# Score columns gathered behind the second half of a projection, one clip per tile, and the first stage's Relu placed behind other copies

## The chip, the cores and the metric

The kernel runs on one core of one Trainium2 chip. A core has five engines that run side by side, each with its own instruction queue: TensorE (PE in the profile; PEld is its weight load), VectorE (DVE), ScalarE (ACT), GpSimd (POOL) and SyncE (SP), which here only issues transfers. ScalarE and GpSimd issue transfers too. The metric is the device time of one execution in microseconds; lower is better.

## What is computed

Four graph layers over 3327 nodes with 512 features each, and one adjacency matrix `adj` for all. Every layer normalises its input, applies a Relu, and adds the layer's output to its input. Layers 0 to 2 are attention layers (8, 4 and 8 heads), layer 3 is a mean over neighbours. An attention layer, cut to what matters here:

```python
h  = maximum(layernorm(x), 0)
Wh = h @ W                          # per head: 64 or 128 columns
s1 = (Wh * a1).sum(-1)              # per node and head
s2 = (Wh * a2).sum(-1)
e  = leaky_relu(s1[:, None] + s2[None, :], 0.2)
x  = x + elu(softmax(where(adj > 0, e, -inf)) @ Wh)
```

The scores s1 and s2 are linear in h, so the kernel folds the vectors a1 and a2 into extra columns of the weight matrix ("score columns"): one projection of a tile of nodes gives Wh and both scores of every head.

## The kernel before, in words

**Tiles and stages.** The nodes lie in 26 tiles of 128. A first stage (to about 150 us) takes layer 0's tiles through normalisation and projection. Then three attention stages follow, each over 7 chunks of four tiles and all heads; the tiles of the next layer are normalised and projected in between, as each chunk gets done, by the same functions. Layer 3 ends it.

**Order.** The program is written as if one thing followed another; a scheduler places the instructions of each engine in an order of its own, from the dependencies and from priorities by place in the source, before the kernel runs. On the chip each engine then goes through its list in that order. The helper `after(inst, name)` (line 145) adds a dependency for the scheduler alone: `inst` has to be placed behind the named instruction. It adds no wait by itself, but the engine's order carries it.

**A tile's steps in the first stage** (`node_stages`, line 530, with `first=True`; line numbers as in the profile):

- load of x (L153, issued from ScalarE's queue); statistics on VectorE (L349, L353), three small operations on GpSimd (L354 to L356);
- Relu with scale and bias on ScalarE, giving `h` (L362);
- four transposes on TensorE into `tp` (L138), a copy on ScalarE into `hT` (L142);
- the projection on TensorE (L418), eight matmuls, into two PSUM tiles `acc` of four that there are: each half `f` of the heads has 256 columns of Wh and 2 x 4 score columns of its own, 264 in all. For tiles 0 and 1 the score columns are made later, by 128x8 matmuls, as their folding (L334, L338) ends late;
- a clip of the scores, one for each half, from PSUM into `s12` on VectorE (L438); two exponentials on ScalarE (L449, L452);
- two multiplications on VectorE (L457), each of one half of Wh with the exponentials, giving `AB`; they free the PSUM tiles;
- `pieces`: AB is split into three bf16 numbers. First pieces are copied on ScalarE (L393, two), the rest `r` is AB minus these, on VectorE (L389), second pieces are copied on ScalarE (L402, two), third pieces are subtracted on GpSimd (L400, two); then they are stored (L410, L411).

The stage is run by a hook that calls one step of each tile in flight, the oldest first. So in one hook run the Relu of tile t + 3 comes after the pieces of tile t in the source. Beside it run the mask steps for the first chunk: a load and cast of `adj` from GpSimd's queue (L227), transposes on TensorE (L235), a comparison on VectorE (L245), a store; and, in the scheduler's gaps, comparison matrices for the first head (L689 on ScalarE, L686, L693 and L695 on VectorE). The attention's matmuls are L804 and L807 (L797 and L800 in layer 1), the last layer's L1073.

**The Relu's place.** In the first stage `relu()` calls `normed` with no named instruction, as `behind()` gives nothing while no attention has run.

Of the kernel before, what the change touches and what calls it, by code (L numbers as in the profile page):

```python
# [25 lines left out]
F32 = mybir.dt.float32  # L26
# [6 lines left out]
ALU = mybir.AluOpType  # L33
# [4 lines left out]
P = 128  # L38
# [14 lines left out]
def tile_gnn(ctx: ExitStack, tc: tile.TileContext, x, adj, W0, a01, W1, al, ar, W2, a2,  # L53
# [91 lines left out]
    def after(inst, name):  # L145

        tc.add_manual_dep(inst.ins, name, mybir.DependencyInfo(mybir.DependencyClass.NoSync,
                                                               mybir.DependencyReason.SCHED_ONLY))
# [10 lines left out]
    stats = []  # L159
    scales = []  # L160
    copied = []

# [132 lines left out]
    def open_layer(l):  # L297
        L = Layer()
        L.l = l
        L.to_store = []  # L300
        if l == 3:
            L.w = []
            for i in range(2):
                w = pre.tile([P, KC, 2 * WW], F32, name="w")[:, :, :D]
                after(nc.sync.dma_start(w, Xd[i].rearrange("(c p) o -> p c o", p=P)), stored["gate"])
                L.w.append(w)
            return L
        H = heads[l]
        DK = D // H
        H2 = H // 2  # L310

        w = pre.tile([P, KC, 2 * WW], F32, name="w")[:, :, :2 * (D // 2 + H)]
        L.w = w.rearrange("p c (f o) -> p c f o", f=2)
        av = []
        for i in range(2):
            av.append(pre.tile([P, 2, H2, DK], F32, name="h"))
            ld = (nc.sync if l or i == 0 else nc.scalar).dma_start(av[i].rearrange("p f h d -> p (f h) d"),
                                                                   a_srcs[l][i].partition_broadcast(P))
            if l:
                after(ld, stored["gate"])  # L320
        for k in range(KC):
            for f in range(2):
                dst = L.w[:, k, f, :D // 2]
                if l == 0:
                    (nc.scalar if f else nc.sync).dma_start(dst.rearrange("p (g o) -> p g o", g=H2),
                                      W0[f * H2:(f + 1) * H2, k * P:(k + 1) * P, :].rearrange("h p o -> p h o"))
                else:
                    W = (W1, W2)[l - 1]
                    ld = nc.sync.dma_start(dst, W[k * P:(k + 1) * P, f * (D // 2):(f + 1) * (D // 2)])  # L329
                    if l:  # L330
                        after(ld, stored["gate"])
        def fold(i, k):
            pr = pre.tile([P, 2, H2, DK], F32, name="e" if l or i else "AB", bufs=1)
            m = (nc.gpsimd if l == 0 and i else nc.vector).tensor_mul(  # L334
                pr, L.w[:, k, :, :D // 2].rearrange("p f (g o) -> p f g o", g=H2), av[i])
            if gone or i:
                after(m, gone[-1] if gone else relus[1])
            nc.vector.tensor_reduce(L.w[:, k, :, D // 2 + i * H2:D // 2 + (i + 1) * H2], pr, AX.X, ALU.add)  # L338
        hooks.small = [lambda i=i, k=k: fold(i, k) for k in range(KC) for i in range(2)]
        L.ks2 = pre.tile([P, NT, H], F32, name="ks2")  # L340
        L.ns2 = pre.tile([P, NT, H], F32, name="ns2")
        L.s12 = pre.tile([P, 2, NT, H], F32, name="s12", bufs=1)
        nc.vector.memset(L.s12, 0.0)
        return L
# [15 lines left out]
    def normed(xt, mv, pool, behind=None):  # L360
        h = pool.tile([P, D], F32, name="h", bufs=2)
        act = nc.scalar.activation(h, xt, AF.Relu, bias=mv[:, 3:4], scale=mv[:, 2:3])  # L362
        if behind:
            after(act, behind)
        relus.append(act.ins.name)
        return h

    def high(v):

        b = v.bitcast(BF16)  # L370
        names = "abcd"[:len(v.shape) - 1]
        return b.rearrange(f"p {' '.join(names[:-1])} ({names[-1]} two) -> p {' '.join(names)} two", two=2)[..., 1]

    def pieces(L, t, AB, pool, first, behind=None):

        l = L.l
        g, jj = jwhere[t]
        H, DA, AO, HW = dims(l)

        o, two = (t % 2, 2) if first else (0, 1)  # L380
        if o == 0:
            L.pt = pool.tile([P, H, 2, two, AO] if l == 1 else [P, H, two, HW], BF16, name="pt", bufs=3 if first else 2)
        pt = L.pt
        def dst(s, a):
            if l == 1:
                return pt[:, :, a, o, s * DA:(s + 1) * DA]
            return pt[:, :, o, a * AO + s * DA:a * AO + (s + 1) * DA]
        r = pool.tile([P, 2, H, DA], F32, name="r", bufs=2 if first else 1)
        sb = nc.vector.tensor_sub(r, AB, high(AB))  # L389
        if behind:  # L390
            after(sb, behind)
        for a in range(2):
            cp = nc.scalar.copy(dst(0, a), high(AB[:, a]))  # L393
            if behind:
                after(cp, behind)
        ones = nc.gpsimd.memset(pt[:, :, :, o, 3 * DA:AO] if l == 1 else
                                pt[:, :, o].rearrange("p h (a w) -> p h a w", a=2)[..., 3 * DA:AO], 1.0)
        after(ones, cp.ins.name)
        for a in range(2):
            nc.gpsimd.tensor_sub(dst(2, a), r[:, a], high(r[:, a]))  # L400
        for a in range(2):
            nc.scalar.copy(dst(1, a), high(r[:, a]))  # L402
        js = slice(jj + 1 - two, jj + 1)
        if o == two - 1 and l == 1:
            for a in range(2):
                L.to_store.append((abd[l][g][:, a, :, js, :].rearrange("h p j w -> p h j w"), pt[:, :, a]))
        elif first and o == two - 1:
            if g not in ahead:
                ahead[g] = pieces_tile(L, bp, g)
            nc.sync.dma_start(ahead[g][:, js], pt[:, 0])  # L410
            stored[t] = nc.sync.dma_start(abd[l][g][:, :, js, :].rearrange("h p j w -> p h j w"), pt).ins.name  # L411
        elif o == two - 1:
            L.to_store.append((abd[l][g][:, :, js, :].rearrange("h p j w -> p h j w"), pt))

    def products(L, pws, hT, o, e):
        for f, pw in enumerate(pws):
            for k in range(KC):
                mm = nc.tensor.matmul(pw[:, o:e], hT[:, k, :], L.w[:, k, f, o:e], start=(k == 0), stop=(k == KC - 1))  # L418
                if o and k == 0:
                    after(mm, L.mm)  # L420
                L.mm = mm.ins.name

    def projected(L, t, hT, first, pws=None):


        l, n = L.l, pn(t)
        H, DA, AO, HW = dims(l)
        H2 = H // 2
        full = D // 2 + H
        if pws:  # L430
            products(L, pws, hT, D // 2, full)
        else:
            pws = [(accs if first else ps).tile([P, full], F32, name="acc" if first else "mm") for f in range(2)]
            products(L, pws, hT, 0, D // 2 if first and t < 2 else full)
            if first and t < 2:
                return pws
        for f, pw in enumerate(pws):
            nc.vector.tensor_scalar(L.s12[:n, :, t, f * H2:(f + 1) * H2],  # L438
                                    pw[:n, D // 2:].rearrange("p (i h) -> p i h", i=2), -S_CLIP, S_CLIP,
                                    op0=ALU.max, op1=ALU.min)  # L440
        return pws

    def scaled(L, t, pws, pool, first, behind=None):

        H, DA, AO, HW = dims(L.l)
        DK, H2 = DA - 1, H // 2
        s2 = L.s12[:, 1, t, :]
        AB = pool.tile([P, 2, H, DA], F32, name="AB", bufs=2 if first else 1)
        ex = nc.scalar.activation(AB[:, 0, :, DK], s2, AF.Exp)  # L449
        if behind:  # L450
            after(ex, behind)
        ex = nc.scalar.activation(AB[:, 1, :, DK], s2, AF.Exp, scale=SLOPE)  # L452
        if behind:
            after(ex, behind)
        for f in range(2):
            hs = slice(f * H2, (f + 1) * H2)
            nc.vector.tensor_mul(AB[:, :, hs, :DK],  # L457
                                 pws[f][:, None, :D // 2].rearrange("p a (h d) -> p a h d", h=H2).to_broadcast([P, 2, H2, DK]),
                                 AB[:, :, hs, DK:DA].to_broadcast([P, 2, H2, DK]))
        return AB  # L460
# [69 lines left out]
    def node_stages(L, t, get_x, pool, first=False):  # L530
# [9 lines left out]

        def relu():

            q["h"] = normed(q["x"], q["mv"], pool, copied[-1] if t == NT - 1 and not first else behind())

        def turn():
            b = L.mm if t == NT - 1 and not first else behind()
# [990 lines left out]
```

## Time and profile before

| | |
|---|---|
| three runs | 3469.95, 3473.6, 3474.15 us; median 3473.6 |
| the profiled execution | 3468.92 us, span 3467.1 us, granted clock of TensorE 0.996 |
| first and last L418 into `acc` (first stage) | 10.1 and 150.8 us |
| first L804 | 151.02 us |
| L457 in the first stage | 26.34 us (tiles 0 and 1) to 154.88 us (tile 25), 0.68 us each |
| L362, mean from 40 to 130 us | 0.81 us |
| L393 and L402, mean of one there | 0.63 us |
| L389, mean there | 1.33 us |
| L400, mean of one there | 1.08 us |
| L438, all of the kernel | 156 of them, some 0.155 us each |

How to read it: the span is the time from the first to the last instruction of one execution that the hardware profiler recorded; the execution's own time has a little around it. A duration in a row includes the engine's latency, so that neighbours on one engine overlap by about 0.1 us. A wait in square brackets is the idle time of the engine just before an instruction, and who ended it. Each projection matmul stands as two records, since float32 goes through TensorE in two passes.

### The profile page before, as it was taken

Reading aid. Unit: us, or ns where it says so; the run is one execution under the profiler, and the core shown is the slowest. Engines: PE = TensorE matmul, PEld = TensorE weight load, DVE = VectorE, ACT = ScalarE, POOL = GpSimd, SP = SyncE. Lnnn points to the kernel's source line nnn. Section 1 sums busy time; section 2 is a strip of 40 time slices with the busy share of each in tenths; the row PEclk is TensorE's granted clock in tenths of the full one; section 3 lists DMA queues with packets and bytes.
Section 4 is the critical chain, followed back from the end, with each engine's and each line's share of the span. In section 5 each row is a group of like instructions: output and inputs, shape, how many; then the busy total and the mean of one; then the engine's idle time right before and its main releaser. Section 6 shows DMA issues by size and latency. Waiting matters only on the chain.

```text
span 3467.1 us, 77643 instructions
## 1 busy us (share of the span) xinstructions
PE 3413.3 (98%) x30751; PEld 3092.9 (89%) x30751; DVE 2638.6 (76%) x5209; ACT 2503.5 (72%) x4125; POOL 640.1 (18%) x894
## 2 busy tenths in 40 slices
PE   8899999999999999999999999999999999999999
PEld 6799999999999788888888879989898989887887
DVE  7889888888878799889988877877776768682221
ACT  6778888878878888888888767766676757582211
POOL 7611222212111202223223320000000001021000
PEclk9999999999999999999999999999999999999999
DMA  8799999999857887887777876555555555486331
GB/s 229 239 294 280 239 265 264 254 271 258 240 186 269 282 290 260 283 277 267 278 271 267 334 271 201 190 189 164 192 174 179 187 175 186 166 299 263 103 110 55
DMA packets 398117, 797.70 MB, mean 230 GB/s; under 512 B 112969, under 2 KB 221844, under 8 KB 397104
## 3 DMA queue, kind: packets, MB, share of 16 engines
q1 hardware_dynamic: 363890, 723.14, 64.9%
q0 software_dynamic: 28128, 62.42, 7.3%
q10 hardware_dynamic: 5726, 7.08, 0.7%
q8 instruction: 245, 4.01, 0.5%
q14 instruction: 128, 1.05, 0.1%
HBM read 663.59 MB, written 129.64 MB: 229 GB/s over the span
## 4 chain that ended last, share of the span: by engine, by line
PE 89%; DMA 3%; DVE 2%; ACT 2%; SPq 1%; issue 0%; POOL 0%; POOLq 0%; DVEq 0%
PE acc L807 25%; PE acc L804 25%; PE acc L797 13%; PE acc L1073 9%; PE acc L800 5%; PE mm L493 5%; PE mm L418 5%; ACT gt L689 1%; PE tp L138 1%; DMA ab<-ab 1%; DMA tr<-at 1%; PE mm L191 1%; DMA ab<-pt 0%; DVE AB L457 0%; SPq L329 0%
## 5 line engine op out<-in xcount | busy, mean ns | idle before, releaser
L689 ACT ACTIVATE gt<-s1b,ks 128x512 fp8e4<-128x512 f32 (+1 forms) x2448 | 1448.4, 677 | 374.8 <-PE acc L807 262.2
L804 PE MATMUL acc<-ab,tht 128*128 128x195 bf16 (+1 forms) x9112 | 1551.8, 248 | 2.4 <-DVE deg L825 1.4
L807 PE MATMUL acc<-ab,gt 128*128 128x195 bf16 (+1 forms) x9112 | 1550.8, 248 | 1.5 <-DVE gt L695 1.5
L807 PEld LDWEIGHTS <-gt 128*128 128x128 fp8e4 x10744 | 1052.2, 98 | 21.4 <-issue 15.4
L804 PEld LDWEIGHTS <-tht 128*128 128x128 fp8e4 x10744 | 1052.3, 98 | 17.2 <-issue 5.8
L693 DVE TENSOR_TENSOR tht<-gt,m 128x768 uint32<-128x768 uint32 (+3 forms) x557 | 448.4, 805 | 100.5 <-ACT gt L689 98.1
L695 DVE TENSOR_TENSOR gt<-tht,m 128x768 uint32<-128x768 uint32 (+3 forms) x557 | 447.3, 803 | 9.5
L658 ACT CAST ts<-tht 128x1536 fp32r<-128x1536 fp8e4 x208 | 302.1, 1471 | 95.9 <-PE acc L797 89.3
L686 DVE TENSOR_SCALAR gt<-s1b,ns 128x512 fp8e4<-128x512 f32 (+1 forms) x446 | 223.7, 505 | 166.7 <-PE acc L807 165.9
L797 PE MATMUL acc<-ab,ts 128*128 128x258 f32 x2496 | 333.1, 289 | 0.2
L797 PEld LDWEIGHTS acc<-ab,ts 128*128 128x128 f32 x2496 | 312.1, 189 | 8.4 <-issue 0.8
L921 POOL TENSOR_TENSOR xt<-xt,e 128x512 f32<-128x512 f32 x72 | 121.2, 1684 | 1047.4 <-DVE e L920 988.5
L689 ACT ACTIVATE tht<-s1b,ks 128x512 fp8e4<-128x512 f32 (+1 forms) x504 | 309.1, 680 | 0.7
L1073 PE MATMUL acc<-y,mf 128*128 128x512 f32 x1352 | 309.6, 391 | 0.0
L1073 PEld LDWEIGHTS acc<-y,mf 128*128 128x128 f32 x1352 | 253.6, 188 | 55.8 <-issue 0.5
L804 PE MATMUL acc<-abx,tht 128*128 128x195 bf16 (+1 forms) x1632 | 283.0, 248 | 1.6 <-DVE tht L693 1.6
L807 PE MATMUL acc<-abx,gt 128*128 128x195 bf16 (+1 forms) x1632 | 283.0, 248 | 0.8 <-DVE rc L842 0.8
L822 DVE TENSOR_REDUCE R<-acc 128x130 f32<-128x390 f32 x416 | 214.7, 555 | 77.8 <-PE acc L807 77.0
L1070 ACT CAST mf<-m 128x768 fp32r<-128x768 fp8e4 (+1 forms) x78 | 59.1, 762 | 243.2 <-PE acc L1073 231.4
L800 PE MATMUL acc<-ab,tht 128*128 128x387 bf16 x1248 | 225.4, 329 | 6.8 <-DMA ab<-ab 5.6
L797 PE MATMUL acc<-ab,tv 128*128 128x258 f32 x1664 | 217.9, 283 | 0.7 <-DMA ab<-ab 0.7
L797 PEld LDWEIGHTS acc<-ab,tv 128*128 128x128 f32 x1664 | 206.9, 189 | 1.4 <-DVE e L905 0.9
(168 smaller groups left out, 3721.9 us busy)
## 6 DMA issues: line engine op xcount, KB each, us to landing
ab<-ab SPq DMA_DIRECT2D x333, 600.0 KB, 5.8
ab<-ab SPq DMA_DIRECT2D x112, 774.0 KB, 6.7
ab<-ab SPq DMA_DIRECT2D x112, 516.0 KB, 5.6
ab<-ab SPq DMA_DIRECT2D x112, 400.0 KB, 3.8
abx<-ab SPq DMA_DIRECT2D x110, 400.0 KB, 6.6
ab<-ab SPq DMA_DIRECT2D x56, 582.0 KB, 6.2
s1b<-s SPq DMA_DIRECT2D x120, 256.0 KB, 5.4
m<-mask SPq DMA_DIRECT2D x69, 384.0 KB, 4.3
```

The lines of the kernel that those rows point to most:

```text
L418: mm = nc.tensor.matmul(pw[:, o:e], hT[:, k, :], L.w[:, k, f, o:e], start=(k == 0), stop=(k == KC - 1))
L658: (nc.scalar.copy if KIND[g] == "s" else nc.vector.tensor_copy)(t[:, :k1 - k0, :nj], th[a][g][:, k0:k1])
L686: nc.vector.tensor_scalar(gv[:, :, jj, :], s1v, L.ns2[:, j, h:h + 1], 2.0, op0=ALU.is_gt, op1=ALU.mult, saturate=False)
L689: nc.scalar.activation(gv[:, :, jj, :], s1v, AF.Relu, bias=L.ks2[:, j, h:h + 1], scale=BIG, saturate=False)
L693: nc.vector.tensor_tensor(pu, gu, mu, ALU.bitwise_and)
L695: nc.vector.tensor_tensor(gu, pu, mu, ALU.bitwise_xor)
L797: mm = nc.tensor.matmul(acc[k][:, :2 * DA], thr[g][:, k - ks[0], jj, :], ab[a][g][:, jj, :], start=(j == 0), stop=(j == NT - 1), skip_grou ...
L800: mm = nc.tensor.matmul(acc[k][:, :3 * DA], th[a][g][:, k, jj, :], ab[a][g][:, jj, :3 * DA], start=(j == 0), stop=(j == NT - 1), skip_grou ...
L804: nc.tensor.matmul(acc[k][:, :3 * DA + o], th[0][g][:, k, jj, :], ab[0][g][:, jj, :3 * DA + o], start=(j == 0), stop=False, skip_group_che ...
L807: mm = nc.tensor.matmul(acc[k][:, AO:AO + 3 * DA + o], th[1][g][:, k, jj, :], ab[0][g][:, jj, AO:AO + 3 * DA + o], start=False, stop=(j == ...
L822: nc.vector.tensor_reduce(R[:, k], v.rearrange("p a (s d) -> p a d s", s=3), AX.X, ALU.add)
L1073: nc.tensor.matmul(acc[k], mf[:, jj, :], y2[g][:, jj, s, :], start=(j0 + jj == 0 and s == 0), stop=(j0 + jj == NT - 1 and s == 1))
```

## The change

Three things are done together.

1. The score columns of all heads stand behind the second half's 256 columns of Wh instead of behind each half's own. The second half becomes 256 + 2 x 8 = 272 columns wide (264 in layer 1 with 4 heads), the first half 256. The weights' layout in SBUF follows, and so does the folding of a1 and a2 (L338).
2. The second half is projected first, then the first half, and the multiplications L457 follow that order. All scores are clipped by one instruction per tile. For tiles 0 and 1 the score columns are one group of four matmuls of 16 columns each instead of two of four with 8 columns.
3. In the first stage the Relu gets a scheduling dependency: it is placed behind the last copy of second pieces (L402) that stands ahead of it in the source.

```diff
@@ open_layer
-        w = pre.tile([P, KC, 2 * WW], F32, name="w")[:, :, :2 * (D // 2 + H)]
-        L.w = w.rearrange("p c (f o) -> p c f o", f=2)
+        L.w = pre.tile([P, KC, 2 * WW], F32, name="w")
...
-                dst = L.w[:, k, f, :D // 2]
+                dst = L.w[:, k, f * (D // 2):(f + 1) * (D // 2)]
...
-            nc.vector.tensor_reduce(L.w[:, k, :, D // 2 + i * H2:D // 2 + (i + 1) * H2], pr, AX.X, ALU.add)
+            nc.vector.tensor_reduce(L.w[:, k, D + i * H:D + (i + 1) * H].rearrange("p (f g) -> p f g", f=2), pr, AX.X,
+                                    ALU.add)
@@ pieces
         for a in range(2):
-            nc.scalar.copy(dst(1, a), high(r[:, a]))
+            cp = nc.scalar.copy(dst(1, a), high(r[:, a]))
+        pieced.append(cp.ins.name)
@@ products, projected
-    def products(L, pws, hT, o, e):
-        for f, pw in enumerate(pws):
-            for k in range(KC):
-                mm = nc.tensor.matmul(pw[:, o:e], hT[:, k, :], L.w[:, k, f, o:e], start=(k == 0), stop=(k == KC - 1))
-                if o and k == 0:
-                    after(mm, L.mm)
-                L.mm = mm.ins.name
+    def products(L, pw, hT, o, e, behind=None):
+        for k in range(KC):
+            mm = nc.tensor.matmul(pw, hT[:, k, :], L.w[:, k, o:e], start=(k == 0), stop=(k == KC - 1))
+            if behind and k == 0:
+                after(mm, behind)
+            L.mm = mm.ins.name
...
         if pws:
-            products(L, pws, hT, D // 2, full)
+            products(L, pws[1][:, DH2:], hT, D, D + 2 * H, L.mm)
         else:
-            pws = [(accs if first else ps).tile([P, full], F32, name="acc" if first else "mm") for f in range(2)]
-            products(L, pws, hT, 0, D // 2 if first and t < 2 else full)
+            pws = [(accs if first else ps).tile([P, DH2 + 2 * H * f], F32, name="acc" if first else "mm")
+                   for f in range(2)]
+            if first and t < 2:
+                products(L, pws[1][:, :DH2], hT, DH2, D)
+            else:
+                products(L, pws[1], hT, DH2, D + 2 * H)
+            products(L, pws[0], hT, 0, DH2)
             if first and t < 2:
                 return pws
-        for f, pw in enumerate(pws):
-            nc.vector.tensor_scalar(L.s12[:n, :, t, f * H2:(f + 1) * H2],
-                                    pw[:n, D // 2:].rearrange("p (i h) -> p i h", i=2), -S_CLIP, S_CLIP,
-                                    op0=ALU.max, op1=ALU.min)
+        nc.vector.tensor_scalar(L.s12[:n, :, t, :], pws[1][:n, DH2:].rearrange("p (i h) -> p i h", i=2),
+                                -S_CLIP, S_CLIP, op0=ALU.max, op1=ALU.min)
@@ scaled
-        for f in range(2):
+        for f in (1, 0):
@@ node_stages, relu
-            q["h"] = normed(q["x"], q["mv"], pool, copied[-1] if t == NT - 1 and not first else behind())
+            b = (pieced[-1] if pieced else None) if first else copied[-1] if t == NT - 1 else behind()
+            q["h"] = normed(q["x"], q["mv"], pool, b)
```

In the built program the Relus of tiles 2 and 3 stand behind the second pieces of tile 1, and from then on that of tile t + 3 behind those of tile t. In the order that the build gives, ScalarE's list for a tile in the first stage changes from

```
exponentials(t+1), copy hT, Relu(t+4), load, first pieces(t+1), second pieces(t+1)
```

to

```
first pieces(t), second pieces(t), Relu(t+3), load, exponentials(t+1), copy hT, first pieces(t+1)
```

and in some groups two tiles' exponentials stand together ahead of both tiles' pieces. VectorE's list moves the mask comparison from before the multiplications to between them and `r` in most tiles, and has one clip fewer per tile; the first mask loads on GpSimd stand behind the third pieces of tiles 0 and 1. On TensorE the transposes of tiles 2 and 3 keep their place behind the score columns of tiles 0 and 1. From the attention on, the lists are the same but for the projection's shapes, the missing clips, and a few neighbours that change places where a layer ends.

More of the change, by code (lines that the diff above doesn't have):

```diff
@@ L161, in tile_gnn @@
     copied = []
+    pieced = []
     WW = D // 2 + 8
@@ L334, in fold @@
             m = (nc.gpsimd if l == 0 and i else nc.vector).tensor_mul(
-                pr, L.w[:, k, :, :D // 2].rearrange("p f (g o) -> p f g o", g=H2), av[i])
+                pr, L.w[:, k, :D].rearrange("p (f g o) -> p f g o", f=2, g=H2), av[i])
             if gone or i:
                 after(m, gone[-1] if gone else relus[1])
-            nc.vector.tensor_reduce(L.w[:, k, :, D // 2 + i * H2:D // 2 + (i + 1) * H2], pr, AX.X, ALU.add)
+            nc.vector.tensor_reduce(L.w[:, k, D + i * H:D + (i + 1) * H].rearrange("p (f g) -> p f g", f=2), pr, AX.X,
+                                    ALU.add)
         hooks.small = [lambda i=i, k=k: fold(i, k) for k in range(KC) for i in range(2)]
@@ L428, in projected @@
         H2 = H // 2
-        full = D // 2 + H
+        DH2 = D // 2
         if pws:
-            products(L, pws, hT, D // 2, full)
+            products(L, pws[1][:, DH2:], hT, D, D + 2 * H, L.mm)
         else:
-            pws = [(accs if first else ps).tile([P, full], F32, name="acc" if first else "mm") for f in range(2)]
-            products(L, pws, hT, 0, D // 2 if first and t < 2 else full)
+            pws = [(accs if first else ps).tile([P, DH2 + 2 * H * f], F32, name="acc" if first else "mm")
[5 more added lines that the diff above has]
+            products(L, pws[0], hT, 0, DH2)
             if first and t < 2:
                 return pws
-        for f, pw in enumerate(pws):
-            nc.vector.tensor_scalar(L.s12[:n, :, t, f * H2:(f + 1) * H2],
-                                    pw[:n, D // 2:].rearrange("p (i h) -> p i h", i=2), -S_CLIP, S_CLIP,
-                                    op0=ALU.max, op1=ALU.min)
+        nc.vector.tensor_scalar(L.s12[:n, :, t, :], pws[1][:n, DH2:].rearrange("p (i h) -> p i h", i=2),
+                                -S_CLIP, S_CLIP, op0=ALU.max, op1=ALU.min)
         return pws
```

## The prediction

> **What bounds the kernel now.** I read the busy shares first, then the windows by stage, then the timeline of one tile and the waits of TensorE. The page:
>
> ```profile
> PE 3413.3 (98%) x30751; PEld 3092.9 (89%) x30751; DVE 2638.6 (76%) x5209; ACT 2503.5 (72%) x4125; POOL 640.1 (18%) x894
> DVE  7889888888878799889988877877776768682221
> POOL 7611222212111202223223320000000001021000
> PE 89%; DMA 3%; DVE 2%; ACT 2%; SPq 1%; issue 0%; POOL 0%; POOLq 0%; DVEq 0%
> ```
>
> TensorE sets the time over the whole, but not at the start, where POOL's first digits are 7 and 6. The windows (TensorE, weight loads, VectorE, ScalarE, GpSimd, then clock, DMA share, GB/s):
>
> ```profile
> 60.00:90.00 30.00, 26.67 (x153) 21.64 (x153) 28.05 (x50) 24.55 (x55) 26.64 (x39) 1.00 0.92 273
> 90.00:120.00 30.00, 26.50 (x143) 21.69 (x143) 29.23 (x55) 25.75 (x56) 27.10 (x47) 1.00 0.90 272
> 120.00:150.00 30.00, 25.06 (x118) 20.27 (x117) 22.60 (x42) 21.11 (x50) 19.87 (x29) 0.89 0.57 193
> 400.00:1000.00 600.00, 600.00 (x6723) 591.40 (x6721) 518.73 (x1036) 497.67 (x847) 117.07 (x181) 1.00 0.96 250
> ```
>
> Up to 150 us, the first stage, VectorE is the fullest engine (28 to 29 of 30 us) and TensorE waits. From 400 to 1000 us TensorE has no idle time. So the change can pay or cost only where the first stage hands over to the attention, at 151.02 us, when L804 first runs. One tile's turn in that stage, from the timeline (start, duration):
>
> ```profile
> 62.69 1.24 DVE L389 TENSOR_TENSOR r<-AB 128x1040 f32<-128x1040 f32 x1
> 63.96 1.16 ACT L402 COPY pt<-r 128x520 bf16<-128x520 bf16 x2
> 64.52 0.94 DVE L245 TENSOR_SCALAR m<-tp 128x768 fp8e4<-128x768 bf16 x1
> 65.18 0.21 ACT L449 ACTIVATE AB<-s 128x8 f32<-128x8 f32 x1
> 65.52 1.29 DVE L457 TENSOR_TENSOR AB<-acc,AB 128x512 f32<-128x512 f32 x2
> 65.85 0.81 ACT L362 ACTIVATE h<-xt,mv 128x512 f32<-128x512 f32 x1
> ```
>
> The subtraction r ends at 63.93, ScalarE copies the second pieces, makes the next tile's exponentials, and VectorE multiplies at 65.52, 1.59 us after r; between them it had the statistics and the mask comparison to do and waited for nothing. The Relu comes after the exponentials. The whole list of multiplication pairs runs from 35.31 (tile 2) to 141.47 (tile 22): 106.2 us for 20 tiles.
>
> **The parts that cost nearly nothing.** Projection columns: eight matmuls of 264 become four of 272 and four of 256, 2112 columns either way, and a tile's take 3.53 us in the chain of waits: difference 0 (layer 1 likewise, 2080 columns from eight of 260 or four each of 264 and 256). One clip replaces two per tile, 78 fewer: at 0.155 us (median row of L438) 12 us of VectorE. 52 of them lie in layers 1 and 2 beside a TensorE without idle time: 0; if that cover were gone, 8 us. The other 26 are 4 us of the first stage, taken into the working below. A clip of twice the width appears in no row; the 8 elements per partition take 0.13 to 0.17 us, so 0.15 up to twice that; I take 0.15, by the row nearest in size. The shuffles elsewhere in the built order (one tile's copies two places earlier, a DMA past its neighbour on SP's queue) touch windows where TensorE idles 14 us in 2000 (1000 to 3000): between -2 and +2, taken as 0. For tiles 0 and 1, the score columns take 8 matmuls for 16, which is 16 records fewer at 4.09/26 = 0.157 us, 2.5 us of TensorE. That would let tile 2's transposes start earlier, but they now wait for something else.
>
> **The Relu, at the start.** It moves behind the second copies of the tile three back (of tile 1 for tiles 2 and 3). Queued behind it on ScalarE: the transposed copy, the next exponentials, hence VectorE's multiplication; behind it on TensorE, the transposes and all that follows them in order.
>
> ```profile
> 22.13 4.09 PE L418 MATMUL acc<-w,hT 128*128 128x8 f32 x26 [1.67 <-DVE w L338]
> 22.72 0.81 ACT L362 ACTIVATE h<-xt,mv 128x512 f32<-128x512 f32 x1 [10.34 <-POOL mv L356]
> 27.84 5.26 PE L418 MATMUL acc<-w,hT 128*128 128x264 f32 x16
> ```
>
> Before, tile 2's Relu ran at 22.72. Now: scores end near 23.8, multiplications and r of tiles 0 and 1 fill 24.0 to 28.8 (four of 0.65, two of 1.2), their four copy pairs on ScalarE (1.06 each) end near 30.2. Relu 0.81, transposes and copy 1.5: projection at 32.7, its second half (8 records at the slow 0.33 of the row above) by 35.4, clip, exponentials: the multiplication at 36.2, against 35.31. Tiles 3 and 4 lose more. On GpSimd the mask loads of tile 0 now stand behind both tiles' third pieces (31 us instead of 23.94), and the built order puts the mask comparison between the multiplication and r, where it needs transposes that stand behind tile 4's and 5's on TensorE. With 0.22 us a record, AB(3) comes at 42.0 (39.39 before) and AB(4) at 48.7 (43.74).
>
> **The Relu, in the steady part.** The built order repeats over three tiles a, b, c. ScalarE: exponentials a and b, P2(a), Relu, first and second copies of b, transposed copy, Relu, exponentials c, copies of c, Relu, exponentials of the next a. VectorE: AB(a), mask, r(a), AB(b), statistics, r(b), mask, statistics, AB(c), mask, r(c), statistics. From AB(a) at 0: AB 1.21, mask 0.9, r 1.24, so r(a) ends at 3.35. AB(b) follows with no wait, r(b) ends 6.4. ScalarE: P2(a) to 4.44 (1.06), Relu to 5.16 (0.58 plus 0.14 of issue in the chain of waits), copies of b to 7.49, transposed copy 0.47, Relu 0.72, and from exponential to multiplication 0.34 (65.18 to 65.52): AB(c) at 9.0. Then r(c) ends 12.4, copies, Relu and exponentials again 2.15: 14.5. VectorE has some 0.8 us of work in that last 2.15 us and idles 1.35. The mask's transposes, behind others on TensorE, add about 0.7: 15.2 for three tiles, 5.08 each. Before, tiles 11 to 16 took 22.76 us, 4.55 each.
>
> Sum: 48.7 + 6 x 15.2 to tile 22, plus three comparison blocks (the two masking operations of an early matrix: 4.13, 2.90 and 2.52 us before, mean 3.2) less the idle 1.35, 5.6; plus 1.4 for one early comparison of 2.83 beyond its idle; less 6 x 0.28 for the shorter last masks: 145.2, against 141.47. End: r(22) 147.8, P2 148.9, transposed copy, Relu(25) done 150.2, its transposes 150.8, and 28 projection records behind them at 0.22: attention at 157.0 against 151.02, **+6.0 us**.
>
> ```profile
> PE acc L804 <- DVE tht L693: 1.6, 1, 1.6
> PE acc L807 <- DVE gt L695: 1.5, 1, 1.5
> 80.11 3.18 DVE L693 TENSOR_TENSOR w<-w,m 128x768 uint32<-128x768 uint32 x1
> 80.39 2.07 POOL L400 TENSOR_TENSOR pt<-r 128x520 bf16<-128x520 f32 x2
> ```
>
> The first two lines, waits of TensorE from 150 to 420 us, are what may be given back: VectorE's last multiplication moves less (near 157.2 from 154.88, +2.3) than TensorE's start, so these 3.1 us may vanish: 0 to 3, I take 1.5. Net **+4.5 us**. The profiled execution took 3468.92 (span 3467.1), giving 3473.4; the median of the runs is 3473.6, so 3478 on that scale.
>
> The Trainium skill speaks against the change at the last two lines above. The masking operation took 3.18 us beside a GpSimd subtraction and 0.93 without one (120.00 us). "SBUF — State Buffer", section "Who interferes with whom", says a VectorE instruction with two SBUF inputs and a GpSimd one that reads SBUF exclude each other for the whole instruction. The row differs in one thing: the one that began first was the one stretched. In the new order all three blocks stand right behind r, when GpSimd takes up its two subtractions; by the rule each would cost 4.1, three times 0.9 more, 3481 in all.
>
> **The rivals.** *Slower, 3488.* ScalarE has no slack left in the loop, and the 16 early comparisons (0.62 each between starts) that the build puts between exponentials and P2 all lengthen it: 9.9 us on top of 4.5. For it: in the new order four of them stand ahead of P2(5), with about 1 us of room in each of two gaps. Against: most stand where ScalarE waits for AB or r. It decides from the point where P2 starts over 0.1 us after r's end in most tiles. *Faster, 3462.* ScalarE's loop is shorter than I count and TensorE sets the pace: 4.39 us a tile (62.99 to 67.38 between mask transposes), 24 tiles from 32.7 with 1.5 for the slow clock end at 139.6, 11.4 earlier. For it: before, VectorE stood idle 2.72 us for exponentials behind two Relus at 55.83 and 3.60 at 130.93, and ScalarE 4.25 behind GpSimd at 126.68; such jams would go. Against: the Relu stands on the way from r to the next exponentials in two tiles of three. *Nothing shows:* TensorE's later waits absorb it all, 3474; this is inside the forecast.
>
> **How the numbers follow.** What a measurement here can tell from no change is about 0.2%, 7 us. The forecast (0 to +7, or a little faster) has 0.45, the slower rival 0.37, since every neglected conflict lengthens the loop, the faster one 0.18. The time is 3478. Its own range: 0 to 3 us given back, 2 either way from the later layers, the three blocks at 2.52 to 4.13 each (2 less to 2.8 more), so 6 - 3 - 2 - 2 = -1 to 6 + 2 + 2.8 = 10.8, or 3473 to 3484. To hold 8 times in 10 it reaches to the slower rival with 1 to spare, 3489, and to two thirds of the faster one's gain, 3466, which leaves out some 2 in 10.
>
> **What would show it.** Right: AB(2) near 36, plain groups of three tiles in about 15 us, VectorE waiting for the exponentials (L449, L452 before) once or twice in three tiles, attention starting at 155 to 159. Wrong: a start before 151 (ScalarE was no loop), or a start there with a total that differs by more than 3 us (then the layers behind matter, which I put at 0).

## The result, and the profile after

The changed kernel took 3483.95 us (median, 3479.53 to 3486.93), the kernel before 3469.95 on the same chip: ratio 1.0034, 95% interval [1.0025, 1.0044]. It is slower by 12 us by the ratio (14 between the two medians). The forecast was 3478, or +4.5; each execution of a kernel differs a little from the next (the changed one spread over 7.4 us), so the ratios rest on all of them, while every stretch and wait below comes from the one that was traced.

The page of the changed kernel: busy time (1), two engines' busy tenths (2), the chain that ended last (4).

```profile
PE 3415.1 (98%) x30735; PEld 3094.1 (89%) x30735; DVE 2636.2 (76%) x5131; ACT 2504.5 (72%) x4125; POOL 638.8 (18%) x894
DVE  7789888888878799889888878867777767682221
POOL 6611222112111202222323320000010000021000
PE 91%; DVE 3%; ACT 3%; DMA 1%; issue 1%; POOL 0%; SPq 0%; ACTq 0%; POOLq 0%; DVEq 0%
```

The work is the same to a few microseconds on every engine: VectorE has 78 instructions fewer and 2.4 us less to do. The 15.1 us between the two spans are idle time and clock. The windows that answer to those shown ahead of the change (TensorE, weight loads, VectorE, ScalarE, GpSimd; then granted clock, DMA share, GB/s):

```profile
60.00:90.00 30.00, 25.39 (x143) 20.82 (x142) 25.73 (x45) 21.39 (x47) 24.14 (x40) 0.94 0.92 275
90.00:120.00 30.00, 25.06 (x122) 20.20 (x122) 24.69 (x39) 23.09 (x50) 20.71 (x41) 0.89 0.85 253
120.00:150.00 30.00, 27.51 (x147) 22.69 (x147) 26.99 (x48) 24.44 (x53) 24.18 (x37) 1.00 0.65 193
400.00:1000.00 600.00, 600.00 (x6722) 591.40 (x6720) 516.54 (x1019) 497.81 (x848) 116.25 (x179) 1.00 0.96 252
```

Up to 120 us no engine is full any more: VectorE falls from 28 or 29 of 30 us to 25 or 26. That is the look of a loop in which several engines wait for each other in turn. The clock is below 1.00 there, which it was not before.

The time by stage, from the first and last matmuls of each group. The kernel before was traced a second time, so that one execution's chance can be seen:

| stretch, us | before | before again | after |
|---|---|---|---|
| start to layer 0's attention | 151.0 | 152.8 | 162.2 |
| from there to layer 1's first projection | 195.2 | 194.4 | 191.8 |
| to the end of layer 0's attention | 822.9 | 822.8 | 822.9 |
| first hand-over, to layer 1's matmuls on real columns (L797, then L802) | 32.3 | 32.6 | 36.7 |
| to the last of these | 812.6 | 814.6 | 814.3 |
| second hand-over and the start of layer 2, to the first matmul of the last projection (L493, then L497) | 215.8 | 215.8 | 217.3 |
| to the last matmul of layer 3 (L1073, then L1078); 8.4 more to the end in all three | 1228.9 | 1229.0 | 1228.6 |

So 11.2 (or 9.4) us are lost in the first stage, about 3 come back at once, and the rest is lost again where layers 1 and 2 take over, where I had put 0.

The predicted steps can be read in the timeline. The start, with the two Relus behind the copies of tiles 0 and 1:

```profile
29.48 0.63 ACT L403 COPY pt<-r 128x520 bf16<-128x520 bf16 x1
30.00 1.51 ACT L363 ACTIVATE h<-xt,mv 128x512 f32<-128x512 f32 x2
30.87 1.97 PE L138 MATMUL tp<-ident,h 128*128 128x128 f32 x8 [7.35 <-ACT h L363]
32.66 5.54 PE L419 MATMUL acc<-w,hT 128*128 128x272 f32 x15
37.24 0.69 DVE L461 TENSOR_TENSOR AB<-acc,AB 128x512 f32<-128x512 f32 x1 [0.38 <-ACT AB L456]
```

TensorE stands 7.35 us for them. One turn of the loop, a tile in which the Relu is on the way:

```profile
84.43 1.23 DVE L390 TENSOR_TENSOR r<-AB 128x1040 f32<-128x1040 f32 x1
85.70 0.63 ACT L403 COPY pt<-r 128x520 bf16<-128x520 bf16 x1 [0.81 <-DVE r L390]
86.23 0.62 ACT L403 COPY pt<-r 128x520 bf16<-128x520 bf16 x1
86.76 0.81 ACT L363 ACTIVATE h<-xt,mv 128x512 f32<-128x512 f32 x1
87.47 0.20 ACT L453 ACTIVATE AB<-s 128x8 f32<-128x8 f32 x1
88.28 1.26 DVE L461 TENSOR_TENSOR AB<-acc,AB 128x512 f32<-128x512 f32 x2
```

r, second copies, Relu, exponentials, multiplication stand in series, as forecast: 2.62 us from r's end to the multiplication, against 1.59 before.

### The profile page after: what moved, and what is told of

Read it like the earlier page. It is cut to its first block, busy times and chain, and to the rows that moved or that the text cites. A ratio compares the mean times of both kernels' runs of the same rounds, so it can differ in the third digit from the quotient of the medians.

```text
span 3482.2 us, 77531 instructions
## 1 busy us (share of the span) xinstructions
PE 3415.1 (98%) x30735; PEld 3094.1 (89%) x30735; DVE 2636.2 (76%) x5131; ACT 2504.5 (72%) x4125; POOL 638.8 (18%) x894
## 4 chain that ended last, share of the span: by engine, by line
PE 91%; DVE 3%; ACT 3%; DMA 1%; issue 1%; POOL 0%; SPq 0%; ACTq 0%; POOLq 0%; DVEq 0%
PE acc L812 25%; PE acc L809 25%; PE acc L802 13%; PE acc L1078 9%; PE acc L805 5%; PE mm L497 5%; PE mm L419 5%; ACT gt L694 1%; PE acc L419 1%; PE tp L138 1%; PE mm L192 1%; DMA ab<-ab 1%; DVE AB L461 1%; DVE r L390 1%; ACT pt L403 0%
## 5 line engine op out<-in xcount | busy, mean ns | idle before, releaser
L802 PE MATMUL acc<-ab,ts 128*128 128x258 f32 x2496 | 333.3, 289 | 0.7 <-DMA ab<-ab 0.6
L802 PEld LDWEIGHTS acc<-ab,ts 128*128 128x128 f32 x2496 | 312.8, 190 | 8.7 <-issue 1.6
L1078 PE MATMUL acc<-y,mf 128*128 128x512 f32 x1352 | 309.6, 391 | 0.0
L1078 PEld LDWEIGHTS acc<-y,mf 128*128 128x128 f32 x1352 | 253.6, 188 | 55.8 <-issue 0.5
L802 PE MATMUL acc<-ab,tv 128*128 128x258 f32 x1664 | 217.9, 283 | 0.0
L401 POOL TENSOR_TENSOR pt<-r 128x520 bf16<-128x520 f32 (+1 forms) x116 | 141.8, 1242 | 359.8 <-DVE r L390 345.0
```

The costliest lines, as they stand in the source:

```text
L802: mm = nc.tensor.matmul(acc[k][:, :2 * DA], thr[g][:, k - ks[0], jj, :], ab[a][g][:, jj, :], start=(j == 0), stop=(j == NT - 1), skip_grou ...
L1078: nc.tensor.matmul(acc[k], mf[:, jj, :], y2[g][:, jj, s, :], start=(j0 + jj == 0 and s == 0), stop=(j0 + jj == NT - 1 and s == 1))
```

## The experiments

In the tables "attention" is the start of layer 0's attention; the hand-overs are the two stretches of the table above (before: 32.3 and 32.6, then 215.8). Ratios are to the kernel before on the same chip; 0.001 is 3.5 us. A ratio stands on 5 to 11 executions, attention and hand-overs on the traced one alone. In f2 this was the fastest of eleven (3476.64 us, median 3482.79), in f5 and g3 the slowest, so a few us between two kernels in those columns can be luck.

**One half of the change at a time, and two forms of the rule**

`e1_columns` keeps the new columns and gives Relu its old place; `e2_relu` is the kernel before with the new rule; `e3_one_older` and `e4_late_rule` are the changed kernel with

```diff
-b = (pieced[-1] if pieced else None) if first else ...
+b = (pieced[-2] if len(pieced) > 1 else None) if first else ...   (e3)
+b = (pieced[-1] if t > 5 else None) if first else ...              (e4)
```

> The changed kernel without the Relu's new place: the gathered score columns, the second half first and the single clip alone. Loop theory (the Relu between second pieces and next exponentials on ScalarE costs all of it): ScalarE's order is the one of before, VectorE has one clip less per tile and the first score matmuls are halved, so the first L804 kind of matmul at 147 to 151 us (before 151.0, changed 162.2) and 3464 to 3471 us in all (before 3470, changed 3484). Rival (the columns' order costs it, since both PSUM tiles are now freed in the opposite order and the wide clip comes late): attention at 158 us or later, 3478 us or more.

> The kernel before with the Relu's new place alone. Loop theory: first attention matmul at 160 to 165 us, total 3480 to 3488 us, as the changed kernel or a little more, since it keeps two clips per tile. Rival (columns): attention at 150 to 152, 3468 to 3473 us.

> The changed kernel with the Relu placed behind the second pieces of one tile further back. The built order then has the exponentials of the next tile ahead of the Relu again, while the start still has tile 2's Relu behind the second pieces of tile 1's neighbours. Loop theory: the pace of before returns (AB pairs 4.4 to 4.6 us apart in plain stretches), only the late start stays, attention at 151 to 157 us, total 3469 to 3478. Rival (any place behind second pieces costs the same): attention near 162, 3484.

> The changed kernel with the Relu's new place only from tile 6 on; tiles 2 to 5 stand as before. Loop theory with the terms of the prediction: the start's 5 us go, the loop stays: attention at 155 to 159 us, total 3475 to 3481. Rival (the late start alone makes the loss and the pace is the same): attention at 150 to 152, total 3468 to 3472.

| kernel | attention | hand-overs | ratio |
|---|---|---|---|
| e1 columns alone | 154.0 | 36.6, 216.9 | 1.0020 [1.0010, 1.0031] |
| e2 Relu rule alone | 169.6 | 34.0, 215.8 | 1.0068 [1.0055, 1.0081] |
| e3 one tile older | 154.7 | 37.7, 218.6 | 1.0025 [1.0015, 1.0035] |
| e4 rule from tile 6 on | 156.8 | 36.6, 218.5 | 1.0038 [1.0025, 1.0051] |

e1 missed: the columns alone cost something too, in its trace in the first stage and at both hand-overs. e2 missed on the high side. With the old columns VectorE's clips wait 18.0 us for the projections between 36 and 155 us (after: 7.6). In the old layout a tile's last score columns end with its last matmul; the new columns, made first, take much of the Relu rule's cost away (1.0068 for the rule alone, 1.0034 with the columns). e3's trace came as the loop theory said: with the Relu one tile older, plain tiles start their multiplications 4.2 to 4.5 us apart (54.86, 59.08, 63.54, 67.92), and attention starts 7.5 earlier than in the changed kernel. By its time, 1.0025 against 1.0034, the gain isn't clear of the noise; with the old columns in layers 1 and 2 it is (f5 against f2 below, 0.9996 and 1.0021). e4's attention started 5.4 us earlier than the changed kernel's, which is the start's share as predicted (5.0), but its ratio is not below the changed kernel's; by its time the gain isn't shown.

**Which layer's columns cost**

The layout of weights, matmuls, clips and multiplications is chosen by layer:

```diff
+NEW = (0,)                      (f1, f2, f5)   /   NEW = (1, 2)   (f3)
+    if L.l not in NEW:
+        return projected_old(L, t, hT, first, pws)
```

f1 and f3 have Relu in its old place, f2 the changed kernel's rule, f5 the rule of e3.

> The new columns in layer 0 alone, Relu as before. In the traces the columns-alone kernel had lost 6.6 us by the end of layer 0 and another 3.8 and 3.4 us where layers 1 and 2 take over. Theory A (the later loss comes from the changed projections of layers 1 and 2, whose built order puts the fusion's transposes ahead of the data of W_self): attention starts at 153 to 155, TensorE's wait for W_self at the first hand-over falls from 3.2 to about 0.3, the clock there is 1.00, and the time is 7 below columns alone: 3469 to 3473, within 0.1% of before. Theory B (the loss was the clock or chance): W_self may be waited for or not, the time stays at 3476 to 3480, 0.2% above before.

> The changed kernel with the columns of layers 1 and 2 as they were before; the Relu rule stays. Theory A: the start and loop are as in the changed kernel (attention at 160 to 164), and the 5 to 7 us of the two hand-overs are gone: 3475 to 3480, 0.15% above before. Theory B: no difference to the changed kernel, 3481 to 3486, 0.34% above before.

> The new columns in layers 1 and 2 alone; the first stage as before, so attention at 150 to 152 and the first matmul behind it near 346. Theory A: TensorE waits some 3 us for W_self at the first hand-over and some 2 us at the second, with a lower clock behind each, and the time is 5 to 7 above before: 3476 to 3480. Theory B: as before, 3470 to 3474.

> The new columns in layer 0 alone, and the Relu behind the second copies of the tile before (one older than in the change). With columns in all three layers this rule gave 3478. Theory A: attention at 154 to 156, nothing lost at the hand-overs, 3470 to 3474, within 0.1% of before. Theory B: 3476 to 3480.

> The kernel before, unchanged, for a second trace. Theory A (the 0.3 us that TensorE waited for W_self at the first hand-over belongs to the kernel before): 0.3 to 0.6 us again, and 32 to 33 us from the end of layer 0's attention (1169.1 in the first trace) to layer 1's first matmul on real columns (1201.4). Theory B (it was that execution's luck, as kernels with the old columns in layers 1 and 2 waited 2.1 to 3.0): 2 to 3 us, and 34 to 37 us between the two. Under both, attention starts at 150 to 152 and GpSimd's wait for nothing else changes.

| kernel | attention | hand-overs | ratio |
|---|---|---|---|
| f1 columns, layer 0 | 154.6 | 36.6, 215.8 | 1.0004 [0.9995, 1.0013] |
| f2 the same and the rule | 157.8 | 35.1, 215.9 | 1.0021 [1.0012, 1.0030] |
| f3 columns, layers 1 and 2 | 149.5 | 37.0, 217.0 | 1.0013 [1.0004, 1.0022] |
| f5 layer 0, one tile older | 153.1 | 36.5, 215.8 | 0.9996 [0.9987, 1.0005] |
| g1 before, second trace | 152.8 | 32.6, 215.8 | one time, 3472.22 |

Theory A holds by the times. Taking the new columns out of layers 1 and 2 gains 0.0016 (e1 to f1), 0.0013 (after to f2) and 0.0029 (e3 to f5); putting them there alone costs 0.0013. That is about 5 us by three of the four pairs and 10 by the other, with intervals of 3 to 5 us either way on each: after to f2 alone is not clear of nothing, the four together are. What in the new columns costs it (the layout, the order of the halves or the single clip) was not separated. Two of A's signs missed: TensorE's wait for W_self did not fall to 0.3, and f2's attention came earlier than 160.

The second hand-over shows it without overlap: 215.8 or 215.9 in all traces with the old columns there, 216.9 to 218.6 in the five with the new ones. There, and at the first hand-over, TensorE also runs the "fusion", products of layer 3's weights (W_self is one) that are made ahead of time (L191, after the change L192). The waits of TensorE from 2000 to 2060 us, two lines of before and one of after (total, count and longest at the end):

```profile
PE mm L191 <- DVE AB L457: 0.3, 1, 0.3
PE mm L191 <- ACT hT L142: 0.2, 1, 0.2
```

```profile
PE mm L192 <- ACT hT L142: 2.2, 2, 2.0
```

The fusion's matmuls now stand where they wait 2.0 us for ScalarE's copy of their transposes (1.7 to 2.0 in the five, 0.2 in the nine). At the first hand-over the mechanism that I had named is only partly right. TensorE's wait there, in the changed kernel, f1 and g1:

```profile
PE tp L138 <- DMA xt<-in_L_gnn_W_self_dram: 3.3, 1, 3.3
```

```profile
PE tp L138 <- DMA xt<-in_L_gnn_W_self_dram: 2.5, 1, 2.5
```

```profile
PE tp L138 <- DMA xt<-in_L_gnn_W_self_dram: 0.6, 1, 0.6
```

f1 has the old columns and the old order there, and waits all the same. The kernel before waits 0.3 and 0.6 in its two traces, every other kernel 1.3 to 3.7, whichever part of the change it has; why the load of W_self then lands later stays open. The whole stretch is 36.6 to 37.7 us in the five traces with the new columns in layer 1 and 32.3 to 36.6 in the nine with the old ones, f1 with 36.6 among them, so here the two overlap. In the changed kernel the wait ends at 1203.02. The windows around it, before, after and f1:

```profile
1200.00:1210.00 10.00, 10.00 (x68) 8.20 (x67) 7.95 (x22) 9.85 (x11) 3.04 (x5) 1.00 0.90 301
```

```profile
1200.00:1210.00 10.00, 6.98 (x16) 3.26 (x17) 6.04 (x12) 5.42 (x11) 0.86 (x2) 0.83 0.76 236
```

```profile
1200.00:1210.00 10.00, 10.00 (x33) 5.49 (x32) 7.84 (x16) 8.47 (x11) 1.17 (x2) 0.87 0.78 265
```

In the changed kernel TensorE idles 3 us, which is that wait, and runs at 0.83 of its clock behind it. f1, with the old columns, has its wait just ahead of this window (until 1198.79) and a lower clock behind it too, so neither belongs to the new columns alone.

**Why columns in layer 0 alone gain nothing**

In e1 and f1 the built order of SP's queue puts the store of the first early scores behind tile 3's piece stores, and both mask stores ahead of the scores' way back. In the timeline of f1:

```profile
44.00 0.25 ACT L563 COPY s1t<-mm 32x128 f32<-32x128 f32 x1
47.06 2.18 SPq L564 DMA_DIRECT2D s<-s1t  x1
56.37 0.89 SPq L738 DMA_DIRECT2D s1b<-s  x2
60.91 0.72 ACT L726 ACTIVATE w<-s1b,ks 128x512 fp8e4<-128x512 f32 x1 [4.44 <-DMA s1b<-s]
```

Before, the store was issued at 42.09 and the first load at 47.66, and the early comparison on ScalarE waited 1.82. Behind it the next tile's copies and exponentials wait. The edit that issues this store earlier, alone (g2) and with the one-older rule from tile 6 on (g4); g3 is g4 without it. All three have new columns in layer 0 only.

```diff
-(nc.sync if first else nc.gpsimd).dma_start(s1d[L.l][c]...
+(nc.scalar if first and c == 0 else nc.sync if first else nc.gpsimd).dma_start(s1d[L.l][c]...   (g2, g4)
+b = (pieced[-2] if t > 5 else None) if first else ...                                            (g3, g4)
```

> The new columns in layer 0 alone, Relu as before, and the store of the first early scores issued by ScalarE instead of SP, where the built order had put it behind the piece stores of tile 3 (46.5 to 47.1 us instead of 42.1). Theory A (with columns alone the first stage loses its 3 us to that order: the first early comparison on ScalarE waits 3.5 to 4.4 us for the scores, and the next tile's copies and exponentials behind it): that wait is under 1 us, the eighth multiplication pair starts at 61 to 63 instead of 64, attention at 150 to 152 and the time is 3 below the kernel without this edit: 0.9990 to 0.9998 of before. Theory B (another cause): attention at 153.5 to 155, ratio 1.0002 to 1.0008.

> The new columns in layer 0 alone, and from tile 6 on the Relu behind the second copies of the tile before (one older than in the change). Theory A (start and pace are separate: the rule costs 4 to 5 us while it holds for tiles 2 to 5 and nothing behind them): tile 4's multiplication at 43 to 45, attention at 148 to 152, 3 to 4 below the same rule for all tiles: 3468 to 3472, ratio 0.9985 to 0.9995. Theory B (what the start loses is regained by tile 8 in any case, and the masking blocks set the end): attention at 152 to 155, ratio 0.9995 to 1.0003.

> Both edits: the new columns in layer 0, the one-older rule from tile 6 on, and the early store by ScalarE. Theory A: attention at 146 to 150, 3465 to 3470, ratio 0.998 to 0.999. Theory B: as the kernel with the rule alone, or a little slower for the comparisons that now stand between a tile's first and second copies (0.6 us each): ratio 0.9995 to 1.001.

| kernel | attention | hand-overs | ratio |
|---|---|---|---|
| g2 early store | 150.4 | 33.3, 215.8 | 0.9995 [0.9986, 1.0004] |
| g3 one older from tile 6 | 154.1 | 35.9, 215.8 | 1.0006 [0.9997, 1.0015] |
| g4 both | 148.2 | 34.0, 215.9 | 0.9990 [0.9981, 0.9999] |

The early comparison in g3, and in g4:

```profile
61.67 0.72 ACT L726 ACTIVATE w<-s1b,ks 128x512 fp8e4<-128x512 f32 x1 [8.05 <-DMA s1b<-s]
```

```profile
56.91 0.72 ACT L726 ACTIVATE w<-s1b,ks 128x512 fp8e4<-128x512 f32 x1 [1.65 <-DMA s1b<-s]
```

g3 and g4 differ in one store's queue and in what the build then does with ScalarE's order: attention starts 5.9 us earlier and the ratio falls by 0.0016, with 0.0013 either way. g3 missed its theory A (attention at 148 to 152): putting the older Relu in from tile 6 on gained nothing while that wait stood there. The wait in g2 fell to 2.21 and not under 1, so the size of A's gain came partly from the changed order of ScalarE. By their times g2 and f1 (0.9995 and 1.0004) can't be told apart. g4 is the one version whose interval lies below the kernel before, and only just: 3466.95 us, 0.1% less.

## Why the prediction was right or wrong

The direction was right, and the time lay inside the stated range. What I called likeliest, a change of 0 to +7 us that can't be told from none, did not come: +12 us is beyond it, and just beyond the +10.8 that ended the range of my own sum. Only the widening towards the slower rival kept the range wide enough on that scale, so part of it is luck.

**Right: the start.** Multiplication pairs of tiles 2, 3 and 4 were put at 36.2, 42.0 and 48.7; they came at 37.24, 43.46 and 48.87.

**Right in its pace, not in its share: the loop.** The multiplication of tile 22 was put at 145.2. It came at 147.61 in the changed kernel and at 143.16 in f2, whose first stage has the same built order on ScalarE, GpSimd and SP. Three tiles took 15.05 us (from tile 8 on), 13.95 and 14.24 (from 17 and 20) against the predicted 15.2, and 17.4 to 19.2 in the other groups. That e3's older Relu gives the pace of 4.4 back shows that the Relu between second copies and exponentials sets the pace of the plain groups. Laid against the first trace of the kernel before, though, the forecast's 6.0 us were 0.9 at tile 2, 2.8 from there to tile 22 and 2.3 behind it. The changed kernel lost 1.9, 4.2 and 5.1, and f2 2.4, -0.7 and 5.1. So over 20 tiles the loop as such cost f2 nothing, and f2's sum, 6.8, is near the forecast only because the terms made up for each other. The masking blocks took 2.64, 2.88 and 1.91 us, less than my 3.2, which is further still from the 4.1 each that I had worked out by the Trainium skill ("SBUF — State Buffer", section "Who interferes with whom"); no block here was held that long. In the first block GpSimd was the one that gave way:

```profile
69.81 0.95 DVE L698 TENSOR_TENSOR w<-w,m 128x768 uint32<-128x768 uint32 x1
69.90 3.50 POOL L401 TENSOR_TENSOR pt<-r 128x520 bf16<-128x520 f32 x2 [1.62 <-DVE s L443]
70.80 1.69 DVE L700 TENSOR_TENSOR w<-w,m 128x768 uint32<-128x768 uint32 x1
```

**Too small: the end of the first stage, 157.0.** It was 162.2, and 157.8 in f2. From the multiplication of tile 22 to attention both took 14.6 us, where I had put 11.8 and the kernel before took 9.6 (e3, with the older Relu, 11.6). I gave TensorE its full pace after its waits. The end in the changed kernel:

```profile
147.90 2.06 POOL L401 TENSOR_TENSOR pt<-r 128x520 bf16<-128x520 f32 x2
149.00 2.06 DVE L390 TENSOR_TENSOR r<-AB 128x1040 f32<-128x1040 f32 x1
152.63 0.81 ACT L363 ACTIVATE h<-xt,mv 128x512 f32<-128x512 f32 x1
152.78 2.18 PE L419 MATMUL acc<-w,hT 128*128 128x272 f32 x4 [2.31 <-ACT hT L142]
154.75 1.06 PE L138 MATMUL tp<-ident,h 128*128 128x128 f32 x4
155.61 6.60 PE L419 MATMUL acc<-w,hT 128*128 128x272 f32 x28
```

Four records of projection matmuls took 2.18 us and four transposes 1.06, where they take 1.18 and 0.60 at a granted clock of 1.00; the granted clock was 0.72 from 150 to 156 us. f2 has much the same there (2.04 and 1.06). Also, r took 2.06 instead of 1.24 in both, beside GpSimd's subtraction, which ended at 149.96 in the changed kernel; that the one held the other is read from these times, not tested.

The 4.4 us between the two kernels arose earlier. The same matmuls of the changed kernel, and of f2:

```profile
64.20 2.18 PE L419 MATMUL acc<-w,hT 128*128 128x272 f32 x4 [1.58 <-ACT hT L142]
```

```profile
64.65 1.18 PE L423 MATMUL acc<-w,hT 128*128 128x272 f32 x4 [1.58 <-ACT hT L142]
```

Tile 8 begins 1.7 us later in the changed kernel than in f2 for it (73.23 and 71.53), and two more slow groups at 97.62 and 115.46 (1.81 and 2.18 us; 1.18 in f2) bring the difference to 4.45 at tile 17, where it stays. Such events cost time because the new loop puts TensorE on the path: between 36 and 155 us ScalarE's transposed copy waited 19.2 us for TensorE's transposes in 14 waits (15.4 in f2; 2.7 in the kernel before, 2.9 in e3), which I hadn't listed among the loop's waits.

**Right in kind, small in size: what is given back.** I took 1.5 of 0 to 3; the stretch behind the attention's start shrank by 2.6 to 3.4 us. The two waits of TensorE that I named (1.6 and 1.5) became one of 3.5, so it was not those that vanished.

**Wrong: the step that put the rest of layers 1 and 2 at 0, ±2.** The prediction put it so: the shuffles "touch windows where TensorE idles 14 us in 2000 (1000 to 3000): between -2 and +2, taken as 0". The mean over a long window says nothing of its two hand-overs, where TensorE does wait and its order is what the change moves. There the new columns cost about 5 us by the times of three pairs; the traces put 1.1 to 2.8 us of it at the second hand-over and leave the rest less sure. The prediction's own last test, a total more than 3 us off the attention's start, pointed there (15.1 us between the spans, 11.2 at the start). So what was forecast as a net +4.5 is a first stage that costs 7.3 by time (f2, 1.0021 [1.0012, 1.0030]) and about 5 in layers 1 and 2.

**The rivals.** The slower one (3488) was nearer in time, +14.4 us, but its mechanism did not show: it asked for second copies that start over 0.1 us after r's end in most tiles, and in 15 of the tiles 2 to 23 they start within 0.05 us (85.70 against 84.43 + 1.23). In the other seven they start 0.1 to 1.3 us late, in three of them right behind an early comparison, so ScalarE's comparisons lengthened the loop in few turns. The faster one (3462) would have needed a shorter loop; the changed kernel hasn't got it.

## What to carry to other kernels

An order constraint that puts one engine's next input behind its last output turns two overlapping chains into one in series: count the loop through all engines, and try the constraint one tile further back, where it cost the plain tiles no pace here. A change of tile shapes also re-orders every queue of a scheduled build, so compare the order at each hand-over between layers and on the DMA queues, however full the engine looks in between. Where an engine whose granted clock falls at times comes onto the path, work its cost out once at full and once at half pace.

## What the runs showed of the hardware

In the first stage and at the first hand-over TensorE fell to half its pace (2.18 us for 1.18, 1.06 for 0.60) for stretches of one length: a granted clock of 0.72 over 6 us, 0.83 over 10 us and 0.89 over 15 us (the changed kernel at 150, 1200 and 60 us) each amount to 3.3 or 3.4 us at 0.5. That agrees with the Trainium skill, "TensorE: Matmul & The Clock Gate", section "HAM oscillation — how this bites in real kernels", in its effect, but not in the gap that it warns of: it asks for no idle gap over 3.4 us, and the waits just ahead of the slow matmuls here were 2.31, 3.33 and 1.58 us. Nor does one wait decide it: f2 waited the same 1.58 us at 64.65 and kept its pace. Where a slow stretch falls differs between executions of the same order: the same four records took 1.18 or 2.18 us in f2 and the changed kernel, and the start of attention differed by 4.4 us with it (157.8, 162.2). The kernel before spread over 149.5 to 152.8 (two traces of it and f3, whose first stage is the same). Between VectorE and GpSimd either may be the one that is slowed: at 69.90 GpSimd's pair of subtractions took 3.50 us instead of 2.06 beside the masking operations, at 149.00 VectorE's subtraction took 2.06 instead of 1.24 beside GpSimd's.
